# Keeping every group's tokens in step order for the closing additions, and moving the last of these additions behind the seam comparison

## The chip, the cores and the metric

The kernel runs on one core of one Trainium2 chip. The metric is the device time of one execution in microseconds (us), as a median of several runs. Five engines work side by side: TensorE (PE in the profile; its weight loads are PEld), VectorE (DVE), ScalarE (ACT), GpSimd (POOL) and SyncE (SP), which in this kernel issues nearly all DMAs.

## The reference, cut to what matters

The input x is 8 images of 128 channels and 48 x 48 positions (2304 tokens each), all float32.

```python
# layer 0
x = x + causal_attention(group_norm(x))              # 1x1 projections, leaky relu, masked softmax
# layer 1, on tokens t of shape (8, 2304, 128)
n = ln(t); t = t + softmax(n @ n.T) @ n              # full attention
Wx = ln(t) @ W.T
Wx = (Wx - mean) * rsqrt(var + 1e-5) * gamma + beta  # over all 8 * 2304 tokens
y = 0
for s in range(2304):                                # for all 8 images together
    y = sigmoid(Wx[:, s] + y @ V.T)
    out[:, s] = t[:, s] + y
```

The part that concerns us is the last line: every output token is the state of the recurrence plus the token `t` before the layer norm.

## The kernel before

**Attention.** One stream of TensorE work runs through the 8 images: for each image first the causal attention, then the full attention, each in 6 chunks of 384 tokens. An item of the stream is a score product, an exponential on ScalarE (L1013 or L1214) and, three items later, the product with the values (L1022, L1226); in the full attention some items read turned scores through a DMA instead (L1222). The order of all instructions is written out by hand: class `Stream` keeps an estimated clock and estimated times at which each engine is free, and small chains of steps (norms, residuals, projections) are run between the items when their estimated input is ready. `st.then` books time on an engine, `advance` runs a chain's steps up to a count, `finish` runs all and moves the clock.

**What a chunk of the full attention leaves.** `Full.after` adds a chain of eight steps per chunk: `sums`, `residual` (which makes the tokens t, called t2), `rooted`, `turn_root`, `spread` (writes t2 channel-major to the DRAM tile `t2_d`), `fetch` (reads it back as `t2x`), `product` (the matmul with W, L1319, and the scaling) and `stored` (a ScalarE copy into `wx`, in step order). The last two chunks of the last image take a shorter chain of seven: `keep_last` in place of the DRAM round trip, then `normed`, `back`, `statistics`.

**Step order.** The recurrence doesn't run over 2304 steps. The sequence is cut into 96 segments of LS = 24 steps, which all run at once after 12 warming-up steps; segments are dealt to three groups of SG = 32. A chunk holds 16 segments, so chunks 0 and 1 belong to group 0, 2 and 3 to group 1, 4 and 5 to group 2. At the end the state each segment reached is compared with the state from which its follower began (`seams`, L1512 to L1515); the result becomes `flag`, and a program branch redoes all in a plain way if they differ.

**The additions before.** For group 0, `keep` copies the chunk's t2x on ScalarE into `t2c` in step order (L1339), and after the second chunk `store` writes steps 0 to LM - 1 = 19 to the output and the last four to `t2l_d`. The output is then completed by a GpSimd DMA that accumulates y into it (L1553). For groups 1 and 2 the tokens are loaded from `t2_d` into `t2s` after the attention, in token order, so that step l of segment s lies at s * 24 + l. Then `add_residual` forms two steps at once, 128 x 512, on GpSimd for steps below LM and on VectorE from there on:

```python
engine, pool = (nc.gpsimd, rres) if l0 < LM else (nc.vector, rlast)
r = pool.tile([P, TZ, B, SG], F32, tag="r", name=f"r_{g}_{l0}")
t2 = t2s[g].rearrange("p b (s l) -> p l b s", l=LS)[:, l0 : l0 + TZ] if g else t2l[:, l0 - LM : l0 - LM + TZ]
engine.tensor_add(r, yt, t2)
nc.sync.dma_start(out[g, :, l0 : l0 + TZ], r)
```

In the recurrence's loop a step is a matmul (L1539) and a sigmoid (L1541) for each group in turn. VectorE writes the next inputs into PSUM (L1488 to L1495). The additions for step pair 20 stand in the loop at step 21, those for pair 22 behind the loop, after the seams and `off` (L1558, L1559). Ahead of the loop, `idle` issues small matmuls without use to TensorE, 14 of them while the batch statistics are reduced.

Of the kernel before, what the change touches and what calls it, by code (L numbers as in the profile page):

```python
# [14 lines left out]
F32 = mybir.dt.float32  # L15
# [11 lines left out]
SEG_GROUPS = 3  # L27
# [577 lines left out]
def fast_path(ctx: ExitStack, tc: tile.TileContext, x, pe, w_ffn, out, x_tok, w_qkv, w_pos, v_t, gamma_beta, flag):  # L605
    nc = tc.nc
    B, C, H, W = x.shape
    N = H * W
    P = 128
# [3 lines left out]
    QC = 384  # L613
    NQ = N // QC
# [7 lines left out]
    dpool = ctx.enter_context(tc.tile_pool(name="dram", bufs=1, space=DRAM))  # L622


    LS = N // SEGS
    SG = SEGS // SEG_GROUPS
    SJ = QC // LS
    wx = cpool.tile([P, LS, B, SEGS], F32, tag="wx", name="wx")

    t2_d = dpool.tile([P, B, N], F32, tag="t2_d", name="t2_d")  # L630
    LM = LS - 4

    t2l_d = dpool.tile([P, LS - LM, B, SG], F32, tag="t2l_d", name="t2l_d")

    posb_d = dpool.tile([P, NQ, 3, QC], F32, tag="posb_d", name="posb_d")


# [24 lines left out]
    with ExitStack() as actx:  # L662
# [9 lines left out]
        work1 = actx.enter_context(tc.tile_pool(name="work1", bufs=1))  # L672
# [14 lines left out]
        def chunk_tile(tag, name, holder=None, steps=0, bufs=2):  # L687

            if holder is not None:
                before = holders.setdefault(tag, deque([({}, 0)] * bufs))  # L690
                old, n = before.popleft()
                before.append((holder, steps))
                if "chain" in old:
                    st.advance(old["chain"], n)
            return (work if bufs == 2 else work1).tile([P, QC], F32, tag=tag, name=name)
# [77 lines left out]
        CAUSAL_FAR, FULL_FAR = True, False  # L773
# [161 lines left out]
        def turned_back(src, name):  # L935

            tp = psum_t(name)
            out_ap = tp[:, :QC].rearrange("p (a g r) -> p g a r", a=R, g=QB)
            for g in range(QB):
                nc.tensor.transpose(out_ap[:, g], src[:, ts(g, P)], ident)  # L940
            return tp
# [174 lines left out]
        class Full:  # L1116
# [35 lines left out]
            def store(self):  # L1152
                j, n, t, at = self.to_store.popleft()
                d = dpool.tile([P, R, QB * QB * SQ], F32, tag=f"e_{j}_{n}", name=f"e_{self.b}_{j}_{n}")
                nc.sync.dma_start(d, t.rearrange("p b j m r -> p b (j m r)"))
                self.stored[j, n] = d, max(at, st.now)
# [75 lines left out]
            def after(self, j, o):  # L1232
# [1 line left out]
                cols = ts(j, QC)  # L1234
                c = {}
                last = b == B - 1 and j >= NQ - 2
                far = FULL_FAR and not last
                if far:
                    ot = turn_result(o, f"f_{b}_{j}", c, True)
                    at = st.then(st.now, [("DVE", 0.57)])  # L1240
# [71 lines left out]
                    nc.sync.dma_start(c["scale"], c["rs_d"][0].partition_broadcast(P))  # L1312

                def product():
                    if j < SG // SJ:
                        keep(c["t2x"])
                        st.then(st.now, [("ACT", 0.85)])
                    tp = psum_t(f"wx_{b}_{j}")
                    nc.tensor.matmul(tp[:, :QC], w1T, c["t2x"], start=True, stop=True)  # L1319
                    nc.vector.tensor_mul(c["scale"], tp[:, :QC], c["scale"])  # L1320
                    nc.vector.bn_stats(stats[:, b * NQ + j, :], c["scale"])
# [10 lines left out]

                def keep(t2x):

                    if before is not None:
                        st.finish(before)
                    if j == 0:
                        self.t2c = work1.tile([P, LS, SG], F32, tag="t2c", name=f"t2c_{b}")
                    nc.scalar.copy(self.t2c[:, :, ts(j, SJ)], t2x.rearrange("p (s l) -> p l s", l=LS))  # L1339

                def store():
                    if j == SG // SJ - 1:
                        nc.sync.dma_start(out[0, :, :LM, b, :], self.t2c[:, :LM])
                        nc.sync.dma_start(t2l_d[:, :, b, :], self.t2c[:, LM:])

# [11 lines left out]
                    nc.scalar.copy(wx[:, :, b, ts(j, SJ)], tp[:, :QC].rearrange("p (s l) -> p l s", l=LS))  # L1357

                def keep_last():
                    tt = chunk_tile("turn", f"tt_{b}_{j}", c, 4, bufs=1)  # L1360
                    nc.scalar.copy(tt, turned_back(c["t2"], f"tk_{b}_{j}")[:, :QC])
                    nc.sync.dma_start(t2_d[:, b, cols], tt)

                if last:
                    steps = [
                        (keep_last, 0.35, [("ACT", 0.5)]),
                        (normed, 0.0, [("DVE", 1.1)]),
                        (back, 0.35, [("ACT", 0.5)]),
                        (statistics, QC * US, [("DVE", 0.55), ("ACT", 0.85)]),
                    ]  # L1370
                else:
                    steps = [
                        (turn_root, 0.0, [("DVE", 0.15)]),
                        (spread, 0.0, [("", 10.0)]),
                        (fetch, 0.0, [("", 9.0)]),
                        (product, QC * US, [("DVE", 1.0)]),
                        (stored, 0.0, [("ACT", 0.85)]),
                    ]
# [10 lines left out]
        def idle(tp, n):  # L1389

            for _ in range(n):
                nc.tensor.matmul(tp[:, :P], ident, ident, start=True, stop=True)
# [46 lines left out]
    TZ = 2  # L1439
    TO = [4] + [2] * (G - 1)  # L1440
    assert LS * SEGS == N and WARM % TZ == 0 and LS % TO[0] == 0 and SG * B * TZ == CH
    with ExitStack() as rctx:
        rc = rctx.enter_context(tc.tile_pool(name="rconst", bufs=1))
        rst = [rctx.enter_context(tc.tile_pool(name=f"rst{g}", bufs=4 if g == 0 else 6)) for g in range(G)]
        rres = rctx.enter_context(tc.tile_pool(name="rres", bufs=6))
        rlast = rctx.enter_context(tc.tile_pool(name="rlast", bufs=3))
        ps_z = [rctx.enter_context(tc.tile_pool(name=f"ps_z{g}", bufs=2, space=PSUM)) for g in range(G)]
        ps_w = rctx.enter_context(tc.tile_pool(name="ps_w", bufs=1, space=PSUM))

        rctx.enter_context(tc.manual_schedule())  # L1450


        t2s = [None] + [rc.tile([P, B, SG * LS], F32, tag=f"t2s_{g}", name=f"t2s_{g}") for g in range(1, G)]
        for g in range(1, G):
            for b in range(0, B, 4):
                nc.sync.dma_start(t2s[g][:, b : b + 4], t2_d[:, b : b + 4, ts(g, SG * LS)])
        t2l = rc.tile([P, LS - LM, B, SG], F32, tag="t2l", name="t2l")
        nc.sync.dma_start(t2l, t2l_d)

# [6 lines left out]
        for t in range(-WARM, -WARM + 2 * TZ, TZ):  # L1466
            for g in range(G):
                z = ps_z[g].tile([P, TZ, B, SG], F32, tag="z", name=f"z_{g}_{t}")
                nc.tensor.matmul(z.rearrange("p t b s -> p (t b s)"), zero[:, :P], zero, start=True, stop=True)
                banks[g].append(z)  # L1470
        idle(pw[:, 2 * P :], 14)

        mv = rc.tile([P, 2], F32, tag="bn_mv", name="bn_mv")
        nc.vector.bn_aggr(mv, stats)
# [34 lines left out]
        def seams(g):  # L1509

            n = SG if g < G - 1 else SG - 1
            nc.vector.tensor_sub(d[:, g, :, : SG - 1], prev[g][:, :, : SG - 1], warm[g][:, :, 1:])  # L1512
            if n == SG:
                nc.vector.tensor_sub(d[:, g, :, SG - 1 :], prev[g][:, :, SG - 1 :], warm[g + 1][:, :, 0:1])
            nc.vector.tensor_reduce(dm[:, g : g + 1], d[:, g, :, :n], AX.XY, ALU.max, apply_absolute_value=True)  # L1515

        def add_residual(g, l0, yt):
            engine, pool = (nc.gpsimd, rres) if l0 < LM else (nc.vector, rlast)
            r = pool.tile([P, TZ, B, SG], F32, tag="r", name=f"r_{g}_{l0}")
            t2 = t2s[g].rearrange("p b (s l) -> p l b s", l=LS)[:, l0 : l0 + TZ] if g else t2l[:, l0 - LM : l0 - LM + TZ]  # L1520
            engine.tensor_add(r, yt, t2)  # L1521
            nc.sync.dma_start(out[g, :, l0 : l0 + TZ], r)

# [6 lines left out]
        for t in range(-WARM, LS):  # L1530
            s = t % TZ
            for g in range(G):
                if s == 0 and t + TZ < LS:
                    zs[g].append(inputs(g, t + TZ))
                so = t % TO[g]
                if so == 0:
                    y[g] = rst[g].tile([P, TO[g], B, SG], F32, tag="y", name=f"y_{g}_{t}")
                z = zs[g][0]
                nc.tensor.matmul(z[:, s], vT_f, prev[g], start=False, stop=True, skip_group_check=True)  # L1539
                to = warm[g] if t == -1 else y[g][:, so]  # L1540
                nc.scalar.activation(to, z[:, s], AF.Sigmoid)  # L1541
                prev[g] = to
                if t == -1 and g == 0:
                    nc.vector.memset(warm[0][:, :, 0:1], 0.0)
                if s == TZ - 1:
                    zs[g].popleft()

                    l0 = t + 1 - TZ
                    if 0 <= l0 and (g or l0 >= LM):
                        if t < LS - 1:  # L1550
                            add_residual(g, l0, y[g][:, so + 1 - TZ : so + 1])
                    elif l0 >= 0 and so == TO[0] - 1:
                        nc.gpsimd.dma_start(out[0, :, t + 1 - TO[0] : t + 1], y[0], accum_op=ALU.add)  # L1553
                if t == LS - 1:
                    seams(g)

        off = rc.tile([P, 1], F32, tag="off", name="off")
        nc.vector.tensor_reduce(off, dm, AX.X, ALU.max)  # L1558
        nc.vector.tensor_scalar(off, off, STATE_TOL, None, ALU.is_gt)  # L1559
        for g in range(G):  # L1560
            add_residual(g, LS - TZ, y[g][:, TO[g] - TZ :])
            if g:
                continue
            nc.tensor.matmul(pw[0:1, P : P + 1], off, ones[:, 0:1], start=True, stop=True)
            nc.vector.tensor_scalar(flag, pw[0:1, P : P + 1], fl[:, 1:2], 0.5, ALU.add, ALU.is_gt)
# [56 lines left out]
```

## Time and profile before

| | |
|---|---|
| time, median of 3 runs | 1782.08 us (1781.37 to 1783.71) |
| span of the profiled run | 1780.2 us |
| TensorE busy, to 1757.8 us | nearly throughout; 98% of the span |
| VectorE, ScalarE, GpSimd busy | 74%, 41%, 12% |
| the attention's stream ends, last chunk's chain begins | about 1697 us |
| first step of the recurrence on TensorE | 1710.80 us |
| last matmul of the recurrence | 1757.76 us |
| last addition ends | 1772.83 us |

Times are counted from the first instruction. So the kernel has one long stretch of 1700 us in which TensorE sets the time, a recurrence of some 47 us, and after it 22 us in which TensorE has one tiny product left. A row of the profile names a source line, an engine, an operation and the tiles `out<-in`; the releaser behind an arrow is what ended an engine's idle time.

### The profile page before, as it was taken

To read this page: it belongs to the slowest core of one execution; us is meant where nothing else is said; L and a number is where in the kernel's file an instruction comes from. 1 tells how busy PE (TensorE), PEld (TensorE's weight loads), DVE (VectorE), ACT (ScalarE), POOL (GpSimd) and SP (SyncE) were. 2 spreads that over 40 slices of the span, in tenths; PEclk is the share of its full clock that TensorE was granted. 3 is DMA by queue.
4 is the path that set the end of the run, shared out by engine and by line. 5 is a ranking of instruction groups with operands and counts; after the bars stand their busy time and mean duration, and the time that the engine had idled before them with its cause. 6 is when DMAs were issued, how large, how long until landed. Compare 5 with 4: busy or idle time off the path is not lost.

```text
span 1780.2 us, 22179 instructions
## 1 busy us (share of the span) xinstructions
PE 1743.5 (98%) x6242; PEld 1093.8 (61%) x6243; DVE 1312.9 (74%) x3361; ACT 735.2 (41%) x1812; POOL 204.9 (12%) x305
## 2 busy tenths in 40 slices
PE   8999999999999999999999999999999999999995
PEld 5666566665666566665666656665666656665574
DVE  4868668866878668786688668786687866876477
ACT  2344424543345423443245433454234442454354
POOL 1110011000110001100110001100011001100026
PEclk8999999999999999999999999999999999999998
DMA  4405662257424584057722574235830576125857
GB/s 142 135 23 191 181 196 90 88 179 196 119 93 133 173 214 125 23 191 191 187 86 89 181 194 121 94 134 164 222 124 23 191 185 179 47 91 180 207 174 200
DMA packets 205576, 256.10 MB, mean 144 GB/s; under 512 B 89889, under 2 KB 175042, under 8 KB 205444
## 3 DMA queue, kind: packets, MB, share of 16 engines
q1 hardware_dynamic: 204492, 251.57, 48.3%
q0 software_dynamic: 720, 2.62, 1.0%
q8 instruction: 52, 0.85, 0.2%
q14 instruction: 80, 0.66, 0.1%
q10 hardware_dynamic: 232, 0.40, 0.1%
HBM read 150.24 MB, written 104.27 MB: 143 GB/s over the span
## 4 chain that ended last, share of the span: by engine, by line
PE 96%; DMA 1%; DVE 1%; issue 0%; ACT 0%; SPq 0%; POOL 0%; ACTq 0%; DVEq 0%; POOLq 0%
PE s L1212 18%; PE o L1226 18%; PE s L1011 17%; PE o L1022 17%; PE o L1222 12%; PE pj L872 4%; PE pj L875 2%; PE z L1539 2%; PE wx L1319 2%; PE tb L932 1%; PE of_t L932 1%; DVE r L1521 0%; PE pb L830 0%; DMA g<-e 0%; DMA x<-in_x_dram 0%
## 5 line engine op out<-in xcount | busy, mean ns | idle before, releaser
L1214 ACT ACTIVATE p<-s,shift 128x384 f32<-128x384 f32 x504 | 292.9, 581 | 486.8 <-PE s L1212 471.5
L1013 ACT ACTIVATE p<-s 128x384 f32<-128x384 f32 (+2 forms) x504 | 232.2, 461 | 440.3 <-PE s L1011 389.4
L1212 PE MATMUL s<-xh 128*128 128x384 f32 x1008 | 410.4, 489 | 0.0
L1226 PE MATMUL o<-p,xhT 128*128 128x384 f32 x1008 | 403.9, 487 | 4.4 <-ACT p L1214 4.4
L1011 PE MATMUL s<-q,k 128*128 128x384 f32 (+2 forms) x1008 | 382.4, 461 | 0.1
L1022 PE MATMUL o<-p,vT 128*128 128x384 f32 (+2 forms) x1008 | 377.8, 457 | 0.0
L1222 PE MATMUL o<-g,xhT 128*128 128x384 f32 x720 | 281.3, 488 | 0.8 <-DMA g<-e 0.8
L1226 PEld LDWEIGHTS o<-p,xhT 128*128 128x128 f32 x1008 | 189.0, 190 | 132.3 <-ACT p L1214 8.7
L1022 PEld LDWEIGHTS o<-p,vT 128*128 128x128 f32 x1008 | 189.0, 191 | 115.0 <-issue 1.1
L1212 PEld LDWEIGHTS s<-xh 128*128 128x128 f32 x1008 | 186.1, 190 | 115.0
L1011 PEld LDWEIGHTS s<-q,k 128*128 128x128 f32 x1008 | 182.8, 191 | 97.2 <-issue 0.6
L1037 DVE TENSOR_TENSOR acc<-acc,p 128x384 f32<-128x384 f32 (+2 forms) x408 | 209.0, 512 | 33.7 <-POOL p L1016 9.1
L1175 DVE STREAM_TRANSPOSE t<-p 128x384 f32<-128x384 f32 x360 | 187.3, 550 | 37.3 <-ACT p L1214 36.1
L1222 PEld LDWEIGHTS o<-g,xhT 128*128 128x128 f32 x720 | 133.2, 190 | 83.2 <-issue 2.2
L1183 DVE TENSOR_REDUCE tsum<-t 128x12 f32<-128x1152 f32 x120 | 162.4, 1353 | 4.2
L877 DVE TENSOR_TENSOR z<-pj,pb 128x384 f32<-128x384 f32 x144 | 78.9, 548 | 110.0 <-PE pj L872 92.0
L1016 POOL TENSOR_TENSOR p<-p,triu 128x128 f32<-128x128 f32 x144 | 72.8, 507 | 607.9 <-ACT p L1013 514.2
L1292 POOL TENSOR_TENSOR roots<-ve_f,mhalf 128x3 f32<-128x3 f32 x48 | 41.1, 856 | 521.0 <-DVE ve_f L916 521.0
L1214 ACT ACTIVATION_READ_ACCUMULATOR p<-s,shift 128x1 f32 x504 | 97.2, 193 | 0.0
L872 PE MATMUL pj<-xn,wT 128*128 128x384 f32 x192 | 79.8, 501 | 1.4 <-DVE xn L865 1.4
L922 POOL TENSOR_TENSOR rs_c<-ve_c,mhalf 128x3 f32<-128x3 f32 x48 | 45.2, 941 | 216.2 <-DVE ve_c L916 213.6
L1320 DVE TENSOR_TENSOR scale<-wx,scale 128x384 f32<-128x384 f32 x46 | 25.4, 552 | 56.3 <-PE wx L1319 56.3
(263 smaller groups left out, 1471.8 us busy)
## 6 DMA issues: line engine op xcount, KB each, us to landing
e<-t SPq DMA_DIRECT2D x120, 576.0 KB
g<-e SPq DMA_DIRECT2D x480, 144.0 KB
pb<-posb_d SPq DMA_DIRECT2D x46, 576.0 KB
t1t<-in_x_tok_dram SPq DMA_DIRECT2D x48, 192.0 KB
t_d<-tt SPq DMA_DIRECT2D x184, 48.0 KB
t2x<-t_d SPq DMA_DIRECT2D x46, 192.0 KB
scale<-rs SPq DMA_DIRECT2D x46, 192.0 KB
x<-in_x_dram SPq DMA_DIRECT2D x14, 576.0 KB
```

Of the source, the lines that this page charges most:

```text
L872: nc.tensor.matmul(ps[:, :QC], wT[:, j, :], xn, start=True, stop=True)
L877: nc.vector.tensor_add(z, ps[:, :QC], c["pb"][:, j, :])
L1011: nc.tensor.matmul(s[:, off:QC], keys[b][:, ts(m, P)], queries[b, j][:, off:], start=True, stop=True)
L1013: nc.scalar.activation(p[:, off:], s[:, off:QC], AF.Exp, scale=SCALE)
L1022: nc.tensor.matmul(o[:, off:QC], vals[b][:, ts(m, P)], p[:, off:], start=first, stop=last)
L1037: nc.vector.tensor_add(a[:, off:], a[:, off:], p[:, off:])
L1175: nc.vector.transpose(t[:, :, :, g, :].rearrange("p b j r -> p j b r"), p.rearrange("p (j b r) -> p j b r", j=QB, b=R))
L1183: nc.vector.tensor_reduce(self.tsum[j][:, n - j - 1, :], t.rearrange("p b j m r -> p (b j) (m r)"), AX.X, ALU.add)
L1212: nc.tensor.matmul(s[:, :QC], xh[:, ts(m, P)], xh[:, ts(j, QC)], start=True, stop=True)
L1214: nc.scalar.activation(p, s[:, :QC], AF.Exp, bias=shift, accum_out=self.rows[:, m, j : j + 1])
L1222: nc.tensor.matmul(out_ap, xhT[:, QB * i + g, :], p, start=first, stop=last)
L1226: nc.tensor.matmul(o[:, :QC], xhT[:, what[1], :], p, start=first, stop=last)
```

## The change

The tokens of all three groups are kept in step order in the way that group 0's were. `product` calls `keep` for each chunk; `t2c`, a single buffer, now serves a pair of chunks of any group, and `store` writes it to a new DRAM tile `t2s_d` for groups 1 and 2. After the attention `t2s` is loaded from there, so that its innermost stretch is 32 neighbouring floats. `keep_last` goes the same way, and no longer writes `t2_d`. `keep` makes sure that the previous chunk's chain has gone far enough. `add_residual` gives VectorE the pair LM - TZ = 18 of groups 1 and 2, at step 21; the pairs 20 and 22 of all groups come behind the seams and `off`. The pool of VectorE's results has four buffers in place of three, and 8 idle matmuls stand where 14 did. (`far` in `Full.after` is reached only with FULL_FAR, which is False, so that edit changes no instruction.)

```diff
+    t2s_d = dpool.tile([P, SEG_GROUPS - 1, B, LS, SG], F32, tag="t2s_d", name="t2s_d")
...
                 def product():
-                    if j < SG // SJ:
-                        keep(c["t2x"])
-                        st.then(st.now, [("ACT", 0.85)])
+                    keep(c["t2x"])
+                    st.then(st.now, [("ACT", 0.85)])
...
                 def keep(t2x):
+                    k = j % (SG // SJ)
                     if before is not None:
-                        st.finish(before)
-                    if j == 0:
-                        self.t2c = work1.tile([P, LS, SG], F32, tag="t2c", name=f"t2c_{b}")
-                    nc.scalar.copy(self.t2c[:, :, ts(j, SJ)], t2x.rearrange("p (s l) -> p l s", l=LS))
+                        st.advance(before, 7 if k else len(before.steps) + before.done)
+                    if k == 0:
+                        self.t2c = work1.tile([P, LS, SG], F32, tag="t2c", name=f"t2c_{b}_{j}")
+                    nc.scalar.copy(self.t2c[:, :, ts(k, SJ)], t2x.rearrange("p (s l) -> p l s", l=LS))
                 def store():
-                    if j == SG // SJ - 1:
+                    g, k = divmod(j, SG // SJ)
+                    if k < SG // SJ - 1:
+                        return
+                    if g:
+                        nc.sync.dma_start(t2s_d[:, g - 1, b], self.t2c)
+                    else:
...
                 def keep_last():
-                    tt = chunk_tile("turn", f"tt_{b}_{j}", c, 4, bufs=1)
-                    nc.scalar.copy(tt, turned_back(c["t2"], f"tk_{b}_{j}")[:, :QC])
-                    nc.sync.dma_start(t2_d[:, b, cols], tt)
+                    keep(turned_back(c["t2"], f"tk_{b}_{j}")[:, :QC])
+                    store()
...
-        rlast = rctx.enter_context(tc.tile_pool(name="rlast", bufs=3))
+        rlast = rctx.enter_context(tc.tile_pool(name="rlast", bufs=4))
...
-                nc.sync.dma_start(t2s[g][:, b : b + 4], t2_d[:, b : b + 4, ts(g, SG * LS)])
+                nc.sync.dma_start(t2s[g][:, b : b + 4], t2s_d[:, g - 1, b : b + 4])
...
-        idle(pw[:, 2 * P :], 14)
+        idle(pw[:, 2 * P :], 8)
...
-            engine, pool = (nc.gpsimd, rres) if l0 < LM else (nc.vector, rlast)
+            engine, pool = (nc.gpsimd, rres) if l0 < LM - TZ else (nc.vector, rlast)
-            t2 = t2s[g].rearrange("p b (s l) -> p l b s", l=LS)[:, l0 : l0 + TZ] if g else t2l[:, l0 - LM : l0 - LM + TZ]
+            t2 = t2s[g].rearrange("p b l s -> p l b s")[:, l0 : l0 + TZ] if g else t2l[:, l0 - LM : l0 - LM + TZ]
...
                     if 0 <= l0 and (g or l0 >= LM):
-                        if t < LS - 1:
-                            add_residual(g, l0, y[g][:, so + 1 - TZ : so + 1])
+                        if l0 < LM - TZ:
+                            add_residual(g, l0, ys[g, l0])
...
                 if t == LS - 1:
                     seams(g)
+                elif t == LM + 1 and g:
+                    add_residual(g, LM - TZ, ys[g, LM - TZ])
...
-        for g in range(G):
-            add_residual(g, LS - TZ, y[g][:, TO[g] - TZ :])
-            if g:
+        for k, (l0, g) in enumerate((l, g) for l in range(LM, LS, TZ) for g in range(G)):
+            add_residual(g, l0, ys[g, l0])
+            if k:
                 continue
```

More of the change, by code (lines that the diff above doesn't have):

```diff
@@ L1236, in after @@
                 last = b == B - 1 and j >= NQ - 2
-                far = FULL_FAR and not last
+                far = FULL_FAR and not (b == B - 1 and j >= NQ - 3)
                 if far:
@@ L1359, in keep_last @@
                 def keep_last():
-                    tt = chunk_tile("turn", f"tt_{b}_{j}", c, 4, bufs=1)
-                    nc.scalar.copy(tt, turned_back(c["t2"], f"tk_{b}_{j}")[:, :QC])
-                    nc.sync.dma_start(t2_d[:, b, cols], tt)
+                    keep(turned_back(c["t2"], f"tk_{b}_{j}")[:, :QC])
+                    store()
                 if last:
                     steps = [
-                        (keep_last, 0.35, [("ACT", 0.5)]),
+                        (keep_last, 0.35, [("ACT", 0.85)]),
                         (normed, 0.0, [("DVE", 1.1)]),
@@ L1450, in fast_path @@
         rctx.enter_context(tc.manual_schedule())
-        t2s = [None] + [rc.tile([P, B, SG * LS], F32, tag=f"t2s_{g}", name=f"t2s_{g}") for g in range(1, G)]
+        t2s = [None] + [rc.tile([P, B, LS, SG], F32, tag=f"t2s_{g}", name=f"t2s_{g}") for g in range(1, G)]
         for g in range(1, G):
             for b in range(0, B, 4):
-                nc.sync.dma_start(t2s[g][:, b : b + 4], t2_d[:, b : b + 4, ts(g, SG * LS)])
+                nc.sync.dma_start(t2s[g][:, b : b + 4], t2s_d[:, g - 1, b : b + 4])
         t2l = rc.tile([P, LS - LM, B, SG], F32, tag="t2l", name="t2l")
@@ L1515, in seams @@
             nc.vector.tensor_reduce(dm[:, g : g + 1], d[:, g, :, :n], AX.XY, ALU.max, apply_absolute_value=True)
+        ys = {}
         def add_residual(g, l0, yt):
-            engine, pool = (nc.gpsimd, rres) if l0 < LM else (nc.vector, rlast)
+            engine, pool = (nc.gpsimd, rres) if l0 < LM - TZ else (nc.vector, rlast)
             r = pool.tile([P, TZ, B, SG], F32, tag="r", name=f"r_{g}_{l0}")
-            t2 = t2s[g].rearrange("p b (s l) -> p l b s", l=LS)[:, l0 : l0 + TZ] if g else t2l[:, l0 - LM : l0 - LM + TZ]
+            t2 = t2s[g].rearrange("p b l s -> p l b s")[:, l0 : l0 + TZ] if g else t2l[:, l0 - LM : l0 - LM + TZ]
             engine.tensor_add(r, yt, t2)
@@ L1548, in fast_path @@
                     l0 = t + 1 - TZ
+                    ys[g, l0] = y[g][:, so + 1 - TZ : so + 1]
                     if 0 <= l0 and (g or l0 >= LM):
-                        if t < LS - 1:
-                            add_residual(g, l0, y[g][:, so + 1 - TZ : so + 1])
+                        if l0 < LM - TZ:
+                            add_residual(g, l0, ys[g, l0])
                     elif l0 >= 0 and so == TO[0] - 1:
```

## The prediction, made before the changed kernel ran

> **What bounds the kernel now.** I read the page first, then the instructions in order of time from 1700 us to the end, VectorE and GpSimd apart, then the groups on tile r, and last the busy time by stretches.
>
> ```profile
> PE 1743.5 (98%) x6242; PEld 1093.8 (61%) x6243; DVE 1312.9 (74%) x3361; ACT 735.2 (41%) x1812; POOL 204.9 (12%) x305
> ...
> L1226 PE MATMUL o<-p,xhT 128*128 128x384 f32 x1008 | 403.9, 487 | 4.4 <-ACT p L1214 4.4
> ...
> L1222 PE MATMUL o<-g,xhT 128*128 128x384 f32 x720 | 281.3, 488 | 0.8 <-DMA g<-e 0.8
> ```
>
> Until about 1700 us the order of TensorE's work is the time: in the whole kernel its products waited 4.4 us for exponentials and 0.8 us for turned scores. There is little for an edit to win there, but something to lose. The end is different:
>
> ```profile
> 1752.17 2.24 DVE L1488 TENSOR_SCALAR z<-wx,bn_a,bn_c 128x512 f32<-128x512 f32 x3 [0.35 <-ACT y L1541]
> 1754.76 6.45 DVE L1521 TENSOR_TENSOR r<-y,t2l 128x512 f32<-128x512 f32 x1 [0.35 <-ACT y L1541]
> 1761.13 5.42 DVE L1521 TENSOR_TENSOR r<-y,t2s 128x512 f32<-128x512 f32 x2
> 1766.47 0.41 DVE L1512 TENSOR_TENSOR d<-y,warm 128x248 f32<-128x248 f32 x1
> ...
> 1769.27 0.15 DVE L1559 TENSOR_SCALAR off<-off 128x1 f32<-128x1 f32 x1
> 1769.34 0.68 DVE L1521 TENSOR_TENSOR r<-y,t2l 128x512 f32<-128x512 f32 x1
> 1769.94 0.20 DVE L1565 TENSOR_SCALAR flag<-pw,fl 1x1 int32<-1x1 f32 x1
> 1770.07 2.76 DVE L1521 TENSOR_TENSOR r<-y,t2s 128x512 f32<-128x512 f32 x2
> ```
>
> Columns: start, duration, then the instruction. One addition 128 x 512 takes 0.68 us at 1769.34 and 6.45 us at 1754.76; the next two take 2.7 us each. The seams stand behind these three on VectorE, and so begin at 1766.47, although the six last sigmoids were done at 1758.18:
>
> ```profile
> 1755.64 2.54 ACT L1541 ACTIVATE y<-z 128x256 f32<-128x256 f32 x6
> ```
>
> So 9 us pass between the recurrence's end and the seams. GpSimd says why:
>
> ```profile
> 1729.34 3.00 POOL L1521 TENSOR_TENSOR r<-y,t2s 128x512 f32<-128x512 f32 x2 [21.34 <-ACT y L1541]
> ...
> 1752.63 7.09 POOL L1521 TENSOR_TENSOR r<-y,t2s 128x512 f32<-128x512 f32 x4
> 1758.54 2.02 POOL L1553 DMA_DIRECT2D out_dram<-y  x1
> 1759.15 6.09 POOL L1521 TENSOR_TENSOR r<-y,t2s 128x512 f32<-128x512 f32 x2
> ```
>
> Its additions start 1.48 us apart, and between 1729.34 and 1765.24 it never rests. Two pairs of steps of the recurrence take 5.18 us (VectorE's groups of inputs are 2.59 us apart); GpSimd needs 4 x 1.48 + 0.6 (one DMA) = 6.5 us for them. It falls behind, and is in the middle of its additions when VectorE begins its own.
>
> [...] 6.45 against 0.68 us; VectorE's three additions and GpSimd's last two end in turn (1761.2, 1762.6, 1763.9, 1765.2, 1766.5). The inputs at L1488 write PSUM from one SBUF source and keep 0.75 us apart beside GpSimd. [...] Here t2s is read with a step of 24 floats. [...] On VectorE the trace itself has both layouts: 1.41 us from t2s, 0.68 from t2l, which is packed.
>
> **The change, part by part.**
>
> *GpSimd.* 18 additions in place of 20, now packed. The trace has no packed one of this size; its nearest row is no help (128x128, 0.5 us[...]), so I bound it: [...] no gain leaves 1.48. I take 1.12. Then two pairs need 4 x 1.12 + 0.6 = 5.1 us against 5.18: it keeps up. The pair 16 is ready at 1729.34 + 8 x 2.59 = 1750.06, and both its additions end by 1752.3; the last DMA of y follows. [...]
>
> *VectorE's pair 18.* Behind the last inputs, which end at 1754.41, it does two additions of 0.6 us (start to start, as at 1769.34): done by 1755.7, in time in which it sat idle or blocked. Seams need y at 1757.3, so this costs nothing. It would still be free with GpSimd at 1.3 us.
>
> *Seams ahead of the additions.* Group 0's last sigmoid is the fourth of the six, ending at 1757.32. The seams and `off` took from 1766.47 to 1769.43, 2.96 us, with their groups' sigmoids 0.43 us apart and thus always ahead. So `off` is done at 1757.35 + 2.96 = 1760.31 in place of 1769.43: 9.1 us earlier.
>
> *The additions behind.* Before: 0.6, flag 0.1, then 1.34 and 1.42 (strided), to 1772.83: 3.4 us. Now six packed ones and the flag: 6 x 0.6 + 0.1 = 3.7 us, if no buffer is waited for. But four buffers serve eight results. The last two need the buffers of the first two behind `off`. An r DMA lands 2.02 us after its issue (1770.05 to 1772.07 in the trace). First addition ends 1760.98, its DMA lands 1763.0; second ends 1761.7, lands 1763.8. The fifth then starts at 1763.05, where it could have at 1762.8; the sixth 1763.8 to 1764.5. So the end of additions moves from 1772.83 to 1764.5: **-8.3 us**. What follows (SyncE's issue 0.65, its load of the flag, the branch, the end) took 7.4 us and depends on SyncE's own order, so it moves along. [...]
>
> *Fewer idle matmuls.* 14 took 3.12 us of pipelined time and ended at 1710.74; 8 take 1.78. The first inputs of group 0 are there at 1709.06, so the first step can start 1.34 us earlier. But VectorE has 2.46 us of inputs per pair of steps against 2.59, and its next inputs only move from 1711.16 to 1710.85, as they wait no longer for TensorE's product L1525. In the second pair group 2's input would be ready at 1713.4, when the step could begin at 1713.15. That keeps 0.28: **-1.07 us**.
>
> *Copies of all chunks.* 30 more ScalarE copies of 1.125 us (two of the 32 take the place of copies to `turn`). In the four stretches around products of chunks 2 to 5, ScalarE is half idle, and exponentials come three items ahead of use:
>
> ```profile
> core 0: us, PE busy (x) PEld busy (x) DVE busy (x) ACT busy (x) POOL busy (x), PEclk, DMA share, GB/s
> ...
> 222.00:230.00 8.00, 8.00 (x31) 4.91 (x30) 5.11 (x12) 2.60 (x8) 0.12 (x1) 1.00 0.94 289
> 247.00:255.00 8.00, 8.00 (x32) 5.26 (x31) 6.47 (x14) 3.85 (x7) 1.10 (x2) 1.00 0.43 125
> 266.00:274.00 8.00, 8.00 (x30) 5.06 (x29) 7.34 (x25) 3.38 (x6) 0.00 (x0) 1.00 0.01 4
> 301.00:309.00 8.00, 8.00 (x30) 4.91 (x29) 5.63 (x21) 3.86 (x7) 0.00 (x0) 1.00 0.12 28
> ```
>
> Behind the copy on ScalarE stand exponentials, and TensorE waits for those. The two copies per image that exist are the measure: one of them is followed by a wait of 0.63 us in seven images, the other never. With ScalarE less busy at the new places I take 0.2 us in all.
>
> *Stores and loads.* 16 stores of 393 KB, less two of 197 KB: 2.3% of 256 MB, behind 0.8 us of waits for g so far: nothing. The loads of t2s keep their 6.3 MB, and ended at 1723, 6 us ahead of the first addition: hidden.
>
> *The new wait.* In the last image `keep_last` of chunk 4 takes t2c again right after chunk 3's store. Before, chunk 3's product was forced by the step behind `keep_last`; now by `keep`. Its t2x landed at 1687.5, so the copy ends about 1688.8 and the store is issued. A t_d store issued at 1688.78 landed at 1691.34; this one is twice as large, so about 1691.9. ScalarE waits for it, with an exponential behind it whose product comes at 1694.3 (not late), and TensorE's next transposes (tx) need the PSUM buffer that this copy reads: 1692.5 in place of 1691.82. **+0.7 us**, between 0 and 2.
>
> Sum: -8.3 - 1.07 + 0.2 + 0.7 = -8.5; 1782.1 - 8.5 = **1773.6 us**.
>
> **Rivals.** (a) [...] GpSimd's addition stays near 1.48 us. 18 of them and four DMAs are 29.2 us and end at 1758.5; VectorE's pair 18 alternates with them and the seams begin 2.5 us late: 1776. For it: no packed addition in the trace. Against it: VectorE's 1.41 to 0.68. (b) *The single t2c costs more*: ScalarE's stall in the last image delays the exponentials too, and the store waits in a full DMA queue (share 1.09 in 1684 to 1690): 2 to 4 us more, 1777. (c) *Slower*: each new copy meets the 0.63 us wait that the first one of an image shows: 30 x 0.63 = 18.9 us, 1792. Against it: the second copy has none. (d) *Better*: no wait at t2c, the chunk's product coming 1.3 us earlier shortens TensorE's 1.64 us wait at tx, and the sixth addition isn't held: 1771.8.
>
> **How the numbers follow.** Forecast 0.62, (a) 0.11, (b) 0.12, (c) 0.05, (d) 0.10. Low end from (d), 1771.5; high end above (b), 1777.6; beyond lie (c) and some of (b). Faster by over 0.2% means below 1778.5: all but (c) and the tail of (b), 0.91; same 0.05; slower 0.04.
>
> **What would show it.** Right: no VectorE addition over 1 us; GpSimd resting between its additions, near 1.1 us apart; seams starting right at the fourth of the last six sigmoids; 7.2 us from there to the end of the last addition; ScalarE waiting for a DMA in front of t2c near 1690. Wrong: GpSimd still 1.4 us apart; waits of products for exponentials well above 4.4 us; the attention's end moved by over 2 us; a chain at the end that runs through landings of r.

## The result, and the profile after

The changed kernel takes 1774.54 us in the median (1773.92 to 1777.68), the kernel before, run beside it, 1782.39 us: a ratio of 0.9959, 95% interval 0.9942 to 0.9976. That is 7.85 us less, where 8.5 were forecast. The profiled runs have spans of 1780.2 and 1772.5 us, 7.7 apart, so the traces can account for the whole.

First the page of the changed kernel, the lines that answer to those shown of before:

```profile
PE 1742.7 (98%) x6231; PEld 1093.2 (62%) x6231; DVE 1302.8 (74%) x3363; ACT 764.8 (43%) x1842; POOL 195.2 (11%) x303
...
L1228 PE MATMUL o<-p,xhT 128*128 128x384 f32 x1008 | 404.1, 488 | 5.9 <-ACT p L1216 5.9
...
L1224 PE MATMUL o<-g,xhT 128*128 128x384 f32 x720 | 281.3, 488 | 1.1 <-DMA g<-e 1.1
```

ScalarE is busy 29.6 us longer (735.2 to 764.8), for the 30 added copies, and the waits of TensorE's products for exponentials grew by only 1.5 us. Then VectorE from the last inputs on, in order of time (start, duration, instruction, idle time before it):

```profile
1752.03 2.24 DVE L1494 TENSOR_SCALAR z<-wx,bn_a,bn_c 128x512 f32<-128x512 f32 x3 [0.35 <-ACT y L1549]
1754.18 2.11 DVE L1529 TENSOR_TENSOR r<-y,t2s 128x512 f32<-128x512 f32 x2
1757.21 0.42 DVE L1518 TENSOR_TENSOR d<-y,warm 128x248 f32<-128x248 f32 x1 [0.92 <-ACT y L1549]
...
1760.02 0.15 DVE L1570 TENSOR_SCALAR off<-off 128x1 f32<-128x1 f32 x1
1760.09 0.68 DVE L1529 TENSOR_TENSOR r<-y,t2l 128x512 f32<-128x512 f32 x1
1760.69 0.20 DVE L1576 TENSOR_SCALAR flag<-pw,fl 1x1 int32<-1x1 f32 x1
1760.82 0.67 DVE L1529 TENSOR_TENSOR r<-y,t2s 128x512 f32<-128x512 f32 x1
1763.39 0.69 DVE L1529 TENSOR_TENSOR r<-y,t2s 128x512 f32<-128x512 f32 x1 [1.90 <-DMA out_dram<-r]
1764.04 0.69 DVE L1529 TENSOR_TENSOR r<-y,t2l 128x512 f32<-128x512 f32 x1
1764.74 0.69 DVE L1529 TENSOR_TENSOR r<-y,t2s 128x512 f32<-128x512 f32 x1
1765.92 0.69 DVE L1529 TENSOR_TENSOR r<-y,t2s 128x512 f32<-128x512 f32 x1 [0.49 <-DMA out_dram<-r]
```

The reader is to see three things. VectorE now waits 0.92 us for the sigmoid ahead of the seams, so these start as early as the data let them. Each packed addition behind the seams takes 0.67 to 0.69 us. And two of the last six wait for a DMA that empties their buffer (1.90 and 0.49 us). GpSimd, in the same view:

```profile
1732.44 5.26 POOL L1529 TENSOR_TENSOR r<-y,t2s 128x512 f32<-128x512 f32 x4
1737.35 1.19 POOL L1562 DMA_DIRECT2D out_dram<-y  x1
...
1749.17 5.96 POOL L1529 TENSOR_TENSOR r<-y,t2s 128x512 f32<-128x512 f32 x4
1754.08 1.88 POOL L1562 DMA_DIRECT2D out_dram<-y  x1
```

Four additions fill the 4.91 us from 1732.44 to 1737.35: 1.23 us each, where 1.48 stood before. That is not fast enough to rest (4 x 1.23 + 0.6 = 5.5 against 5.18 us), but the backlog is small: the last addition ends at 1755.13, not at 1765.24 as before.

The span falls into stretches that can be compared run by run. The columns: from the end of the attention's last product to the end of the recurrence's last matmul; from there to the start of the seams; seams and `off`; to the end of the last addition; to the end of the span; and the sum of the last four. All are differences of two time stamps of a trace, in us, and each row is one profiled execution. The labels e1 to e12 stand for the experiments of the next section.

| run | recurrence | to seams | seams | additions | to the end | tail |
|---|---|---|---|---|---|---|
| before | 60.68 | 8.71 | 2.96 | 3.40 | 7.37 | 22.4 |
| the change | 59.75 | -0.41 | 2.96 | 6.44 | 5.88 | 14.9 |
| e1 layout alone | 59.76 | 2.53 | 2.95 | 2.83 | 7.46 | 15.8 |
| e2 order alone | 59.75 | 4.53 | 2.95 | 7.11 | 5.83 | 20.4 |
| e3 14 idle matmuls | 60.67 | -0.41 | 2.97 | 6.69 | 5.89 | 15.1 |
| e4 eight buffers | 59.76 | -0.41 | 2.97 | 3.72 | 6.75 | 13.0 |
| e7 no last accumulation, two more r | 59.75 | -0.18 | 2.95 | 6.30 | 5.80 | 14.8 |
| e12 no last accumulation | 59.76 | -0.41 | 2.97 | 6.35 | 5.86 | 14.8 |
| e8 three edits | 59.80 | -0.22 | 2.95 | 3.72 | 7.54 | 14.0 |
| e11 before, GpSimd quiet | 60.68 | 0.30 | 2.96 | 5.62 | 6.90 | 15.8 |

Before against after: -0.93 in the recurrence, -7.57 in the tail, and +0.79 in the attention (its last product ended at 1697.08 and 1697.87). The last is no result: over the profiles of this study that moment lay between 1695.0 and 1702.5, and for attention code that was not touched at 1697.1, 1698.0 and 1702.5. So sizes of 1 us are read from the stretches, not from medians. The stretches scatter too. Besides the change, e3, e5 and e6 have the change's instructions behind the recurrence, and these four tails are 14.9, 15.1, 15.0 and 14.3 us, with additions of 6.4, 6.7, 6.5 and 5.9: a difference of tails under 0.8 us tells nothing.

### The profile page after: what moved, and what is told of

Its sections match the earlier page's. It is cut to its first block, busy times and chain, and to the rows that moved or that the text cites. A ratio compares the mean times of both kernels' runs of the same rounds, so it can differ in the third digit from the quotient of the medians.

```text
span 1772.5 us, 22223 instructions
## 1 busy us (share of the span) xinstructions
PE 1742.7 (98%) x6231; PEld 1093.2 (62%) x6231; DVE 1302.8 (74%) x3363; ACT 764.8 (43%) x1842; POOL 195.2 (11%) x303
## 4 chain that ended last, share of the span: by engine, by line
PE 96%; DMA 1%; DVE 1%; ACT 0%; issue 0%; SPq 0%; POOL 0%; ACTq 0%; POOLq 0%; DVEq 0%
PE o L1228 18%; PE s L1214 18%; PE s L1013 17%; PE o L1024 17%; PE o L1224 13%; PE pj L874 4%; PE pj L877 2%; PE z L1547 2%; PE wx L1320 2%; PE of_t L934 1%; PE tb L934 1%; PE pb L832 0%; DMA x<-in_x_dram 0%; PE dn L1072 0%; PE ts L1259 0%
```

## The experiments

**What blocked VectorE before (e11).** The forecast puts VectorE's long additions down to GpSimd's, which ran at the same time. The direct test leaves GpSimd's late additions out, with their reads, writes and stores:

```diff
-                        if t < LS - 1:
+                        if t < LS - 1 and not 14 <= l0 < LM:
                             add_residual(g, l0, ...)      # of the kernel before
```

> The kernel before, with GpSimd's additions of step pairs 14, 16 and 18 of groups 1 and 2 left out (those outputs stay without them); all else as before. Theory [...]: with GpSimd done when VectorE adds pair 20, the three additions take 0.7, 1.4 and 1.4 us in place of 6.5, 2.7 and 2.7, and the seams begin as soon as these are done, near 1758.5, 8 us earlier. Rival (VectorE waits for buffers or transfers): the first addition stays above 4 us.

VectorE in order of time in that run:

```profile
1755.72 0.69 DVE L1521 TENSOR_TENSOR r<-y,t2l 128x512 f32<-128x512 f32 x1 [0.35 <-ACT y L1541]
1756.33 2.77 DVE L1521 TENSOR_TENSOR r<-y,t2s 128x512 f32<-128x512 f32 x2
1759.03 0.41 DVE L1512 TENSOR_TENSOR d<-y,warm 128x248 f32<-128x248 f32 x1
```

The same three instructions take 0.69, 1.43 and 1.43 us (6.45, 2.74 and 2.75 before), and the seams begin 0.30 us after the recurrence's last matmul instead of 8.71. The run took 1776.20 us, a single one. Neither a buffer nor a transfer of VectorE's was changed, so the rival falls: the 8.4 us were GpSimd's additions. Their stores went with them, but busy DMA engines without GpSimd's additions didn't block VectorE: in the change, for 1.5 us behind the seams, GpSimd rests while the DMA engines are busy for 0.95 of the time (0.88 from 1755.0 to 1761.2 before), and VectorE's packed additions take 0.68 and 0.67 us:

```profile
core 0: us, PE busy (x) PEld busy (x) DVE busy (x) ACT busy (x) POOL busy (x), PEclk, DMA share, GB/s
1760.00:1761.50 1.50, 0.19 (x2) 0.09 (x2) 1.47 (x4) 0.00 (x0) 0.00 (x0) 0.75 0.95 257
```

Which part of GpSimd's additions blocked VectorE, their reads or their writes, was not shown: no run here parts them. The 1.43 us that stay are the stride: from packed tokens the same additions take 0.67 to 0.69 us in the change. The additions behind the seams took 5.62 us here because the first of them waited 2.12 us for a buffer.

**Layout alone (e1).** The edit in the changed kernel:

```diff
-            engine, pool = (nc.gpsimd, rres) if l0 < LM - TZ else (nc.vector, rlast)
+            engine, pool = (nc.gpsimd, rres) if l0 < LM else (nc.vector, rlast)
...
-                        if l0 < LM - TZ:
+                        if l0 < LS - TZ:
                             add_residual(g, l0, ys[g, l0])
...
-                elif t == LM + 1 and g:
-                    add_residual(g, LM - TZ, ys[g, LM - TZ])
...
-        for k, (l0, g) in enumerate((l, g) for l in range(LM, LS, TZ) for g in range(G)):
+        for k, (l0, g) in enumerate((l, g) for l in range(LS - TZ, LS, TZ) for g in range(G)):
```

> All of the change but the new order of the additions: GpSimd keeps pair 18, VectorE adds pair 20 in the loop at step 21 ahead of the seams, pair 22 behind them; tokens packed, 8 idle matmuls, four buffers. Theory [...]: GpSimd's additions stay 1.24 us apart, 20 of them and five DMAs end near 1757, so VectorE's pair 20 is blocked again, its first addition takes over 1.5 us, the seams begin near 1758.7 and not at 1757.2, but only three additions follow: last addition's end between 1763.5 and 1767, time 1772 to 1776. Rival (the order is what pays): the three additions cost what they did before, the seams begin past 1763, time near 1779.

Measured: 1774.85 us, ratio 0.9947 (0.9931 to 0.9964). That interval overlaps the change's, so the medians don't tell layout alone from the whole change. VectorE and then GpSimd in order of time:

```profile
1755.72 4.41 DVE L1529 TENSOR_TENSOR r<-y,t2l 128x512 f32<-128x512 f32 x1 [0.35 <-ACT y L1549]
1760.05 1.28 DVE L1529 TENSOR_TENSOR r<-y,t2s 128x512 f32<-128x512 f32 x2
```

```profile
1753.23 2.99 POOL L1529 TENSOR_TENSOR r<-y,t2s 128x512 f32<-128x512 f32 x2
1755.67 1.38 POOL L1562 DMA_DIRECT2D out_dram<-y  x1
1756.28 3.29 POOL L1529 TENSOR_TENSOR r<-y,t2s 128x512 f32<-128x512 f32 x2
```

VectorE's first addition is still blocked, until GpSimd's last one ends at 1759.57. But GpSimd is nearly done by then, so the other two cost 0.6 us apart. The seams come 2.9 us later than with the change, and since only three additions follow them, the additions take 3.6 us less. The tail is 15.8 against 14.9 us: the layout brings 6.6 of the 7.6 us. Up to the end of the last addition it brings all: that end lies 8.3 us behind the recurrence's last matmul here, 9.0 with the whole change and 15.1 before.

**Order alone (e2).** The kernel before with the new order of the additions (the edits of the change in `add_residual`, the loop and behind it), four buffers and 8 idle matmuls; tokens in token order.

> The new order, four buffers and 8 idle matmuls, but the tokens of groups 1 and 2 still in token order (no copies, no stores of them; loads from t2_d). Theory: GpSimd's additions stay 1.48 us apart, 18 of them and four DMAs end near 1758.5, VectorE's two additions of pair 18 are blocked to about 1759, the seams begin 2 us later than with the change, and four of the six last additions take 1.4 us in place of 0.7: last addition's end near 1770, time 1777 to 1779. Rival (the order alone pays): within 1 us of the changed kernel, 1774.5.

Measured: 1779.33 us, ratio 0.9979 (0.9969 to 0.9990). VectorE in order of time:

```profile
1758.84 8.05 DVE L1523 TENSOR_TENSOR r<-y,t2s 128x512 f32<-128x512 f32 x2
1766.81 0.40 DVE L1512 TENSOR_TENSOR d<-y,warm 128x248 f32<-128x248 f32 x1
```

and GpSimd:

```profile
1757.15 7.08 POOL L1523 TENSOR_TENSOR r<-y,t2s 128x512 f32<-128x512 f32 x4
```

The two additions of pair 18, meant to fill idle time, take 8.05 us, as they stand behind four of GpSimd's; the first got through only when all four were done (1764.24). The tail shrinks by 2.0 us only, and 1.5 of these lie behind the last addition. With the layout's 6.6 that makes 8.6, more than the 7.6 together. So the order is worth little by itself. On top of the layout it isn't shown to be worth anything with four buffers: the seams come 2.9 us sooner, but the last addition ends 0.7 us later, as two of the six wait for buffers, and the 0.9 us that the tail is shorter come from behind that addition. With eight buffers (e4, below) the last addition ends 6.3 us behind the recurrence, 2.0 sooner than with the layout alone; there the order pays.

**Fewer idle matmuls (e3).** 14 in place of 8 in the changed kernel.

> The changed kernel with 14 idle matmuls ahead of the recurrence, as before. Theory: the recurrence starts later by what the idle matmuls stood in the way of, 0.5 to 1.1 us; time 1775.0 to 1775.6. Rival: first inputs are late anyway, no difference: 1774.5.

The median, 1774.13 us (ratio 0.9954, 0.9936 to 0.9971), can't tell; the trace can. The recurrence's stretch is 60.67 us with 14 and 59.75 with 8, and it is 60.68 and 59.69 to 59.80 in all other runs with 14 and 8. So the six matmuls cost 0.92 us.

**The copies (e6).** Each copy into t2c made twice:

```diff
                     nc.scalar.copy(self.t2c[:, :, ts(k, SJ)], t2x.rearrange("p (s l) -> p l s", l=LS))
+                    nc.scalar.copy(self.t2c[:, :, ts(k, SJ)], t2x.rearrange("p (s l) -> p l s", l=LS))
```

> The changed kernel with each of the 48 copies into t2c made twice (same data, same place). Theory: ScalarE has room; its busy time rises by 52 us, TensorE's wait for exponentials by under 1.5 us in all, time within 2 us of the changed kernel. Rival (copies cost): each doubled copy adds the 0.63 us that TensorE waits behind the first copy of an image, 20 us or more, 1795.

Measured: 1776.24 us, ratio 0.9959 (0.9944 to 0.9975), the same as the change. On the page ScalarE is busy 814.7 us, 49.9 more, and TensorE's products wait 6.9 us for exponentials where they waited 5.9. 48 more copies cost 1 us of waiting, so the 30 of the change cost none that could be seen, apart from what follows.

**The wait in the last image (e5).** In the changed kernel, ScalarE in order of time:

```profile
1690.75 1.14 ACT L1326 COPY wx<-scale 128x384 f32<-128x384 f32 x1 [0.60 <-DVE scale L1321]
1693.27 0.48 ACT L1341 COPY t2c<-tk 128x384 f32<-128x384 f32 x1 [1.39 <-DMA t2s_d<-t2c]
1693.65 0.59 ACT L1216 ACTIVATE p<-s,shift 128x384 f32<-128x384 f32 x1
```

and TensorE:

```profile
1692.36 0.49 PE L942 MATMUL tx<-ident,x 128*128 128x128 f32 x3
1694.38 0.91 PE L1228 MATMUL o<-p,xhT 128*128 128x384 f32 x2 [1.52 <-ACT p L1216]
```

The single t2c is waited for as forecast (1.39 us), and the exponential behind it is late by 1.52 us. But the transposes tx, for which TensorE waited 1.64 us before, wait no more. The experiment gives chunk 4 of the last image a place of its own:

```diff
+                        if b == B - 1 and j == NQ - 2:
+                            free = big.tile([P, N], F32, tag="x", name="t2c_x")
+                            self.t2c = free[:, : LS * SG].rearrange("p (l s) -> p l s", l=LS)
+                        else:
-                        self.t2c = work1.tile(...)
+                            self.t2c = work1.tile(...)
```

> The changed kernel with a buffer of its own for the last pair of chunks of the last image: chunk 4's t2c lies in the place of the image tile x, which is free by then. Theory (the new wait): ScalarE's wait of 1.4 us for the store of t2c goes, the product behind it no longer waits 1.5 us for its exponential, and between 1690 and 1698 us TensorE's idle time falls by 1 to 1.5 us; time 1773.3. Rival: the wait at the transposes (1.64 us before the change) comes back in its place; TensorE's idle time there stays above 1 us, time 1774.5.

Measured: 1773.31 us, ratio 0.9941 (0.9921 to 0.9961). The copy no longer waits, the product waits 0.27 us in place of 1.52, and the total on the page falls from 5.9 to 4.7. The mechanism is shown; its 1.2 us can't be told in a median.

**Buffers and transfers at the end.** The change's third addition behind the seams waited until 1763.39 for the buffer of pair 18's first result, whose DMA was issued at 1755.76. That transfer took 7.6 us, where one took 2.0 before. The sixth waited for a transfer of 4.31 us, and the chain of work that ended last runs through it (start, duration, what):

```profile
1760.89 0.61 DVE r L1529
1761.50 0.02 issue
1761.52 4.31 DMA out_dram<-r
```

I took GpSimd's accumulating DMA (issued 1754.08) to be in its way. Three runs bear on this: eight buffers in place of four (e4); group 0's steps 16 to 19 added by VectorE, so that the last accumulating DMA goes but two more r are stored (e7); and that DMA left out with nothing in its place, so that these outputs keep the tokens alone (e12).

```diff
-        rlast = rctx.enter_context(tc.tile_pool(name="rlast", bufs=4))      # e4
+        rlast = rctx.enter_context(tc.tile_pool(name="rlast", bufs=8))
...
-    LM = LS - 4                                                            # e7; LM0 in t2l, t2l_d and store
+    LM, LM0 = LS - 4, LS - 8
...
-                elif t == LM + 1 and g:
-                    add_residual(g, LM - TZ, ys[g, LM - TZ])
+                elif t == LM + 1:
+                    for l0 in (LM - TZ,) if g else (LM0, LM - TZ):
+                        add_residual(g, l0, ys[g, l0])
...
-                    elif l0 >= 0 and so == TO[0] - 1:                      # e12
+                    elif l0 >= 0 and so == TO[0] - 1 and t < LM - 1:
```

> The changed kernel with eight buffers for VectorE's results in place of four, so that none of the eight is waited for. Theory: the waits of 1.9 and 0.5 us ahead of VectorE's third and sixth last addition go, the additions behind the flag run 0.6 us apart, the last one ends near 1764.2 in place of 1766.6, and the time falls by 2.4 us to 1772.1. Rival: the results then queue for the same transfers and the end waits for the landing of the last ones: 1774.5.

> The changed kernel with group 0's steps 16 to 19 taken out of GpSimd's last accumulating DMA: t2l holds eight steps in place of four, and VectorE adds pairs 16 and 18 of group 0 at step 21 beside the two it has there. Four buffers, as in the change. Theory (r's transfers stand behind the accumulating DMA): without it r lands 2 us after its issue in place of 7, the third last addition no longer waits, only the fifth and sixth wait under 1 us each; last addition's end 7.3 us after the first seam's start in place of 9.4, time 1772.4. Rival (r's transfers are slow in themselves): the waits stay, 1774.5 or more.

> The changed kernel with GpSimd's last accumulating DMA (group 0, steps 16 to 19) left out, so those outputs hold the tokens alone; no other transfer is added. Theory: VectorE's third last addition doesn't wait for a buffer, the fifth and sixth wait under 1 us each; from the first seam to the last addition's end 7.3 us in place of 9.4. Rival (r's own transfers are the limit): the sum of the waits stays above 2 us.

Eight buffers: 1773.32 us, ratio 0.9947 (0.9930 to 0.9964). No addition waits, the last ends 2.7 us sooner after `off`, and the tail is 1.8 us shorter in this trace. Of the 2.7, 0.9 comes back: SyncE now issues the last DMAs one after the other, and takes up to 0.97 us for one in place of 0.33.

Without the accumulation: e7 1773.56 us, ratio 0.9943 (0.9921 to 0.9966), e12 1773.19 us in a single run. The tail is that of the change, 14.8 us, in both. VectorE in e12:

```profile
1759.63 1.27 DVE L1529 TENSOR_TENSOR r<-y,t2s 128x512 f32<-128x512 f32 x2
1760.83 0.67 DVE L1529 TENSOR_TENSOR r<-y,t2l 128x512 f32<-128x512 f32 x1
1761.73 0.69 DVE L1529 TENSOR_TENSOR r<-y,t2s 128x512 f32<-128x512 f32 x1 [0.23 <-DMA out_dram<-r]
1764.64 0.69 DVE L1529 TENSOR_TENSOR r<-y,t2s 128x512 f32<-128x512 f32 x1 [2.22 <-DMA out_dram<-r]
```

The third addition no longer waits, so the accumulating DMA was what held its buffer: that half of the theory stands. But the sixth starts no sooner. Its wait grew from 0.49 to 2.22 us, since the transfer that it waits for is as slow without the accumulating DMA as with it:

```profile
1760.32 4.22 DMA out_dram<-r
```

The same transfer takes 4.18 us in e7 and 4.31 in the change. So the third addition's wait cost the change nothing at the end, and leaving the accumulating DMA out didn't shorten the additions (6.35 us for 6.44). In this run one of SyncE's issues takes long too:

```profile
1761.53 1.89 SPq L1530 DMA_DIRECT2D out_dram<-r  x1
```

My expectation of waits under 1 us fell. What slows that issue and the transfer is open; e7 has the same issue (1.84 us). The transfer was issued just as three engines branched on the flag (1760.3 here, 1761.5 in the change). The slow issue came some 1.3 us after that, but it is also the fourth of four stores issued 0.6 to 0.7 us apart, and no run separates that.

**Together.** The three edits (spare t2c, no last accumulation, seven buffers: e8), then spare t2c and eight buffers with the accumulation kept (e10), then the first once more (e8b):

> The changed kernel with the spare t2c of the last image, without the last accumulating DMA, and with seven buffers for VectorE's results. Theory: the gains add where they don't overlap: last addition's end 6.7 us after the first seam's start (2.7 less than in the change), 1 us less ahead of the recurrence; time 1771.5. Rival: the end is set by something else than the additions, 1773.

> The changed kernel with the spare t2c of the last image and eight buffers for VectorE's results; group 0's last accumulating DMA stays with GpSimd. Theory: both gains add: the tail from the recurrence's last matmul to the end is 13.0 us as with eight buffers alone, in place of 14.9, and TensorE idles 1 us less in the last chunk; time 1771.5. Rival (what the spare t2c won is noise of the attention): 1772.7.

> The kernel of the run with all three edits once more, timed in more rounds, since single medians of one kernel have moved by 1 to 2 us between chips. Theory (its gain is real): ratio to the kernel before again near 0.9935, a tail of 14.0 us from the recurrence's last matmul to the end, and no wait of TensorE for exponentials in the last chunk. Rival (chance of one chip): ratio near the change's own 0.9959 with the tail still shorter by 0.8 us.

Medians: 1771.15, 1775.15 and 1774.43 us. Ratios: 0.9934 (0.9911 to 0.9956), 0.9961 (0.9946 to 0.9975), 0.9951 (0.9937 to 0.9965). Tails: 14.0, 13.9 and 14.4 us. The first met its expected 1771.5, and its repetition didn't; the second missed by 3.7 us, and its tail is 0.9 us longer than that of eight buffers alone (13.0), though the instructions behind the recurrence are the same. The traces show each gain (no addition waits for a buffer), but the spans hold other things: in the second, TensorE waited 1.25 us ahead of a product of turned scores at 1476 and 0.60 us for t2x at 1690, which no edit touched. All three intervals overlap the change's own. So a version better than the change is likely, by about 1 us in the tail, and isn't shown.

## Why the prediction was right

- *The stretch it chose* was right: the attention's time didn't move beyond its scatter, and 7.6 of the 7.7 us between the two profiles lie behind the recurrence.
- *Blocked additions, seams sooner*: forecast 9.1 us, measured 9.12 (8.71 to -0.41). e11 shows what blocked, and e1 that the layout alone takes 6.2 of it away. (Beside GpSimd the inputs of VectorE start 0.72 us apart, not 0.75 as the forecast read.)
- *GpSimd's addition*: forecast 1.12 us apart, measured 1.23; it didn't quite keep up, and VectorE's first addition of pair 18 took 1.51 us for 0.68. The reserve of 1.6 us ahead of the seams hid that, as the forecast said that it would at 1.3. The 1.12 was the author's estimate, and no trace of before showed it. Measured, the stride cost GpSimd 0.25 us an addition (1.48 against 1.23).
- *The additions behind*: this term was mis-sized. Forecast +0.8 us against before (the last two waiting for a landing 2.0 us after issue), measured +3.04: the third waited 1.90 us and the sixth 0.49. The step that failed is "an r DMA lands 2.02 us after its issue". The one that decided took 4.31 us, and 4.22 without the accumulating DMA (e12), so its cause is open; the one of 7.6 us stood behind that DMA, which I had counted as landed before. The figure of 2.02 was of one of the quickest: the profile of before also has one of 2.80 us, issued at 1758.29.
- *What follows the last addition*: forecast unchanged, measured -1.49 us (7.37 to 5.88). 0.3 is SyncE's last issue (0.65 to 0.33 us); the rest lies behind the branch, where the runs scatter between 4.7 and 6.0 us, and is open. It hid two thirds of the previous error (1.5 of 2.2 us).
- *Idle matmuls*: forecast 1.07, measured 0.93. The step is right in its parts: the first step began 1.34 us earlier after the attention, as forecast, and the recurrence kept 0.93 of it.
- *The new wait*: it came where forecast, with 1.39 us on ScalarE, but cost nothing net: TensorE waited 1.52 us at a product in place of 1.64 us at the transposes. The forecast of +0.7 left to its rival (d) that the chunk's product, now with eight other matmuls between it and the transposes, would end that older wait.
- *Copies and stores*: nothing to be seen, as forecast; doubling the copies cost 1 us of waiting.
- *The rivals*: (a) is refuted by the 1.23 us, (c) by e6; (b), 2 to 4 us more, didn't come: the attention's end stayed within its scatter, and e5 puts the single t2c at 1.2 us; of (d), only the wait at tx went. What the forecast got least clear is the share of the parts: it put the gain down to the order, while the layout alone brings 6.6 us and the order alone 2.0.
- *Its own signs*: two came (the seams start at the fourth of the last six sigmoids, ScalarE waits for a DMA in front of t2c). Three didn't: a VectorE addition took 1.51 us, GpSimd never rested, and from the seams to the last addition's end it was 9.4 us for 7.2. One sign of being wrong came: the chain at the end runs through a landing of r. So it was right that GpSimd's additions held up VectorE's (8.4 us in e11), and the total of -8.5 came close in part by luck, as +2.2 us at the additions met -1.5 us behind them that the forecast didn't have and the runs don't explain.

## What to carry to other kernels

When an elementwise instruction takes many times its usual duration (here 6.45 us for 0.68), look at what the other engines did in that time: here moving work between VectorE and GpSimd brought little (2.0 us of the tail, e2) while GpSimd's additions came 1.48 us apart, and the layout that made it 1.23 brought 6.6 us (e1). Data laid out for the reader at a time when an engine has room for the copy was nearly free here (48 more copies cost 1 us of waiting, e6), and paid at the end, where nothing hides it. When a chain is shortened by issuing stores closer together, don't take their landing time from one of the quickest in the trace (2.02 us, where 4.31 and 7.6 came), and give them buffers enough that nobody has to know it: without that, the new order gained nothing at the last addition (9.0 us behind the recurrence's last matmul, 8.3 with the layout alone).

## What the hardware showed that was not expected

- A VectorE addition that found GpSimd in a run of queued additions was let through only when the run ended: 6.70 us behind four of them in e2, 4.41 us behind the last of them in e1. In the profile of before the first took 6.45 us, and the next two, 2.74 and 2.75 us, took turns with GpSimd's. So in these traces the block lasted for several instructions of GpSimd's, not for one.
- GpSimd's additions 128x512 came 1.48 us apart with one operand at a step of 96 bytes and 1.23 packed; VectorE's took 1.41 and 0.68. The stride cost VectorE more (0.73 us) than GpSimd (0.25).
- The profile's durations on GpSimd grew from 1.27 to 2.29 us within a run while the starts stayed 1.23 us apart, so what an addition cost GpSimd is taken from the starts.
- A DMA issue of r on SyncE mostly took 0.33 us. The longest (1.84 us in e7, 1.85 in e8, 1.89 in e12) each came some 1.3 us after other engines had branched, as the fourth store in a row. The transfer issued at that branch took 4.18 to 4.31 us to land in e7, e12 and the change.
